# A graph kernel's first spreading: slot numbers of the even ranges as 8-bit bands

## The chip, the cores and the metric

The kernel runs on one NeuronCore of one Trainium2 chip. Its time is the device time of one execution in microseconds; of several executions the median is given. Changes of this kernel's time under about 0.2% are treated as no change.

## The reference, cut to what matters

Two layers of a graph network over N = 32768 nodes with D = 128 features and E = 524288 edges. The first layer sums the features of each edge's source at its destination; this sum is what the change touches:

```python
src, dst = (edge_index[0], edge_index[1])
agg = jax.ops.segment_sum(x[src], dst, num_segments=N)
h = (1.0 + eps) * x + agg
h = jax.nn.relu(h @ W_loc1 + b_loc1) @ W_loc2 + b_loc2
h_local = _bn(x + h, g1, beta1)
# beside it: attention of 8 heads over 64 blocks of 512 nodes, then a feed-forward part
```

The second layer does three steps of a retrieval (softmax over 512 keys) with a normalised sum over the same edges. Each layer ends in a layer norm.

## The kernel before, in words

**Ranges and slots.** The nodes are cut into NW = 256 ranges of 128. For each source range w and each of the 256 destination ranges there are KS = 6 slots, so a source range has SL = 2·6·128 = 1536 slots: 12 blocks of 128, six for each half of the destination ranges. A slot holds one edge, by the number (1 to 128) of the source node inside its range, or 0 for none. Edges that find no slot go through lists and are gathered elsewhere.

**Where the slot numbers are made.** `Grid.build` sorts the edges beside the first attention blocks and writes tables to memory: among them `row` of the key `dst`, 1536 slot numbers for each range, in bf16 (L816). For the other key, `src`, the same kind of table is written in 8 bits (`row2`, L824 to L826), and a later stage reads it.

**The stage of the change, `spread_x`.** It runs after the first 52 attention blocks and before a branch, from about 2375 us to 3625 us of the profiled span. The ranges are taken in order. For range w:

- Its one-hot `pick` is a 128 x 1536 tile: row p has a one where the slot number is p + 1. For an odd w the row of slot numbers is read from memory 128 times over, into all partitions (`band`, 384 KB, L1838), and VectorE compares the bf16 tile at once (`pick_b`, L1844). For an even w the row lies in SBUF (`row`, loaded once, L1371); TensorE copies 512 of it at a time to all partitions by a matmul with a column of the identity (`row_p`, L1423), and VectorE compares each of the three pieces from PSUM (`pick`, L1848).
- `spread` multiplies each 128 x 128 block of the one-hot with the 128 x 384 rows of the range (`rows`: x in three bf16 parts). For m = 0 to 5 two matmuls (L1448) fill a PSUM tile `exp` (three of these), and ScalarE or VectorE copies it to the SBUF tile `y_o` (L1453). VectorE has m = 2 of every range and m = 5 of the odd ones; ScalarE has the rest. There are two tiles `y_o`.
- After m = 2 and after m = 5 SyncE's queue issues a store of half the tile to `slots` (L1456, 576 KB each).

Every four ranges the next block of x is loaded (`xe`, L1826, 256 KB) and split in four small steps (L1395 to L1399), the last of which stores `rows`. Between the m of all ranges a share of a second sort is issued (`build_more`, `sort_on`): compares on VectorE, transposes on TensorE, copies on ScalarE. It has a quota in estimated time; its long compares end before 3300 us, and shorter steps follow until the end of the stage.

**Order.** The stage is under a manual schedule: each engine takes its instructions as the Python loop issues them, and waits only where a tile is not ready or not free. All loads and stores of the stage are on SyncE's queue, in issue order. Before the change the order in iteration w is: for odd w the load of the band of w + 2; every fourth w the load of x; and then for each m the two matmuls, the copy, a store after m = 2 and 5, and after m = 1, 3 and 5 one piece of the next range's `pick` (for an odd next range all of it after m = 1).

Of the kernel before, what the change touches and what calls it, by code (L numbers as in the profile page):

```python
# [9 lines left out]
F32 = mybir.dt.float32  # L10
I32 = mybir.dt.int32
BF16 = mybir.dt.bfloat16
FP8 = mybir.dt.float8e4
U8 = mybir.dt.uint8
AF = mybir.ActivationFunctionType
OP = mybir.AluOpType
# [4 lines left out]
P = 128  # L21
D = 128
BLK = 512
# [8 lines left out]
KS = 6  # L32
# [145 lines left out]
class Order:  # L178
# [10 lines left out]
    def __init__(self, tc, name, n, own, ident, iota, lane_f, dram, pool):  # L189
        nc = tc.nc  # L190
        self.tc, self.name, self.n = tc, name, n
        self.own, self.oth = (7, 0) if own == "src" else (0, 7)
        self.ident, self.iota, self.lane_f = ident, iota, lane_f
        self.NW = 2 * P
        self.F = n // P
        self.NS = self.F // self.SUB
        self.table = dram(f"sorted_{name}", (n + WL, 1), I32)
        self.pivots = dram(f"pivots_{name}", (P, self.NS), I32)
        self.begin = pool.tile([P, self.NW + 1], F32, name=f"begin_{name}")
        self.at = pool.tile([P, 2], I32, name=f"at_{name}")  # L200
# [233 lines left out]
class Grid:  # L434
# [18 lines left out]
    def __init__(self, tc, main, over, dram, pool):  # L453
        self.tc, self.main, self.over = tc, main, over
        NW = 2 * P
        self.out = {k: {"slot": dram(f"slot_{k}", (P, NW * self.NC2), BF16),
                        "other": dram(f"other_{k}", (P, NW * OW), I32),
                        "shared": dram(f"shared_{k}", (P, NW // GW * SH), I32),
                        "row": dram(f"row_{k}", (P, 2 * 2 * KS * P), U8 if k == "src" else BF16)}
                    for k in ("src", "dst")}  # L460
        self.more = dram("more", (P, 2, self.over.F // 2), I32)
        self.bad = pool.tile([P, self.NBAD], F32, name="bad")
        tc.nc.vector.memset(self.bad, 0.0)
        self.groups = pool.tile([P, P // GW], F32, name="groups")
        self.earlier = pool.tile([P, P], F32, name="earlier")
# [100 lines left out]
    def build(self, pp):  # L566

        tc, nc, PADL, NC2, Q, OL, LOW = self.tc, self.tc.nc, self.PADL, self.NC2, self.Q, self.OL, self.LOW
        main = self.main
        WS, OS = main.WSHIFT, main.OSHIFT  # L570
        mine, theirs = self.out["dst"], self.out["src"]
        NW = 2 * P
# [4 lines left out]
        with tc.tile_pool(name="gr", bufs=1) as sp:  # L577
# [16 lines left out]
            for h in range(2):  # L594
                with tc.tile_pool(name=f"gr_h{h}", bufs=1) as hp:
# [6 lines left out]
                    with tc.tile_pool(name=f"gr_a{h}", bufs=1) as ap:  # L602
# [13 lines left out]
                        w = ap.tile([P, 1], F32, name="w")  # L616
# [14 lines left out]
                                                op0=OP.is_gt)  # L631
# [50 lines left out]
                    with tc.tile_pool(name=f"gr_c{h}", bufs=1) as ap:  # L682
# [7 lines left out]
                        m = mask[:, :OL]  # L690
# [62 lines left out]
                        w = kept_w[:, :Q]  # L753
                        m = mask[:, :Q]
# [34 lines left out]
                        for b in range(10, -1, -1):  # L789
                            g = 1 << b  # L790
# [17 lines left out]
                        row = ap.tile([P, 2, KS, P], BF16, name="row")  # L808
                        for g in range(2):
# [6 lines left out]
                        nc.sync.dma_start(  # L816
                            mine["row"].rearrange("p (g h f) -> p g h f", g=2, h=2)[:, :, h, :],
                            row.rearrange("p g r w -> p g (r w)"))

                        half = ap.tile([P, KS, 2, P], BF16, name="half")  # L820
                        nc.scalar.copy(half.rearrange("p r g w -> p g r w"), vb)
# [88 lines left out]
def tile_gnn_resnorm(ctx: ExitStack, tc: tile.TileContext, a: dict, out: bass.AP):  # L910
# [8 lines left out]
    nc = tc.nc  # L919
# [3 lines left out]
    NW = N // P  # L923
# [5 lines left out]
    def dram(name, shape, dt=F32):  # L929
        return nc.dram_tensor(name, shape, dt, kind="Internal").ap()  # L930
# [17 lines left out]
    ident = cp.tile([P, P], F32, name="ident")  # L948
# [30 lines left out]
    w = {}  # L979
# [342 lines left out]
    SL = 2 * KS * P  # L1322
# [3 lines left out]
    gc = {}  # L1326
# [11 lines left out]
    def rows_of(t, i):  # L1338

        return t.rearrange("(b c p) d -> b p c d", c=NCH, p=P)[i]  # L1340
# [14 lines left out]
    class Exchange:  # L1355
# [10 lines left out]
            self.width = table.shape[1]  # L1366
            self.bands = {}

        def load_rows(self, pool):
            self.row = pool.tile([P, 2, SL], BF16, name="row")  # L1370
            nc.sync.dma_start(self.row.rearrange("p h f -> p (h f)"), self.grid["row"])  # L1371

        def load_tables(self, pool):

            self.slot = pool.tile([P, NW, NC2, 2], BF16, name="slot")
# [31 lines left out]
        def known_pick(self, wp, w):  # L1407
            pick = wp.tile([P, SL], FP8, name="pick", bufs=3)
            nc.sync.dma_start(pick, pick_d[w])
            return pick  # L1410

        def pick(self, wp, pp, tag, w):

            pick = wp.tile([P, SL], FP8, name="pick", bufs=3)
            for j in range(SL // BLK):
                nc.vector.tensor_scalar(pick[:, j * BLK:(j + 1) * BLK], self.listed_row(pp, tag, w, j), gc["lane1"],
                                        None, op0=OP.is_equal, saturate=False)
            return pick

        def listed_row(self, pp, tag, w, j):  # L1420

            ps = pp.tile([P, BLK], F32, name="row_p", tag=tag)
            nc.tensor.matmul(ps, gc["ident"][:, w % P:w % P + 1].to_broadcast([P, P]),  # L1423
                             self.row[:, w // P, j * BLK:(j + 1) * BLK], start=True, stop=True)
            return ps

        def load_band(self, wp, w):
            if w < NW:
# [383 lines left out]
    def spread_x():  # L1812

        ex = Exchange("dst", slots_d[1], rows_d[T_STEPS])
        with tc.tile_pool(name="l0r", bufs=1) as gp, tc.tile_pool(name="l0e", bufs=2) as wp, \
                tc.tile_pool(name="l0e_p", bufs=2, space=PSUM) as p_k, \
                tc.tile_pool(name="l0e_e", bufs=3, space=PSUM) as p_e:
            grid_consts(gp)
            ex.load_rows(gp)
            xb, rows, ends, picks, bands, y = {}, {}, {}, {}, {}, {}  # L1820
            more = {"steps": grid.build_more(lane, Bank(p_k, "row_p")), "quota": 0.0}

            def load(b):
                if b < NB:
                    xb[b] = wp.tile([P, NCH, D], F32, name="xe", bufs=3)
                    nc.sync.dma_start(xb[b], rows_of(a["x"], b))  # L1826

            def split(b):
                if b < NB:
                    x = xb.pop(b)  # L1830
                    rows[b], ends[b] = ex.split_steps(wp, b, x, x)

            def row_of(w):

                if w < NW:
                    bands[w] = wp.tile([P, SL], BF16, name="band")
                    src = ex.grid["row"][w % P:w % P + 1, w // P * SL:(w // P + 1) * SL]
                    nc.sync.dma_start(bands[w], src.to_broadcast([P, SL]))  # L1838

            def pick(w, j):  # L1840
                if w < NW and w % 2:
                    if j == 0:
                        picks[w] = wp.tile([P, SL], BF16, name="pick_b")
                        nc.vector.tensor_scalar(picks[w], bands.pop(w), gc["lane1"], None, op0=OP.is_equal)  # L1844
                elif w < NW:
                    if j == 0:
                        picks[w] = wp.tile([P, SL], FP8, name="pick")
                    nc.vector.tensor_scalar(picks[w][:, j * BLK:(j + 1) * BLK], ex.listed_row(p_k, "row_p", w, j),  # L1848
                                            gc["lane1"], None, op0=OP.is_equal, saturate=False)

            def sort_on():

                more["quota"] += MORE
                while more["steps"] is not None and more["quota"] > 0:
                    us = next(more["steps"], None)
                    if us is None:
                        more["steps"] = None
                    elif us < 0:
                        more["quota"] = 9 * us * MORE
                    else:  # L1860
                        more["quota"] -= us

            with tc.manual_schedule():
                load(0)
                load(1)
                split(0)
                for f in ends.pop(0):
                    f()
                row_of(1)
                for j in range(SL // BLK):  # L1870
                    pick(0, j)
                for w in range(NW):
                    b, c = divmod(w, NCH)
                    if w % 2:
                        row_of(w + 2)
                    if c == 0:
                        load(b + 2)
                        split(b + 1)
                    for m in range(KS):
                        ex.spread(wp, p_e, "exp", w, picks[w], rows[b][:, c, :], m, y, m == 2 or (m == 5 and w % 2))  # L1880
                        if m % 2:
                            pick(w + 1, m // 2)
                        if m == 3 and b + 1 in ends:
                            ends[b + 1][c]()
                        sort_on()
                for _ in more["steps"] or ():
                    pass
# [403 lines left out]
    with tc.tile_pool(name="atg", bufs=1) as gp, tc.tile_pool(name="ata", bufs=2) as ap, \  # L2291
# [4 lines left out]
        with tc.manual_schedule():  # L2296
# [13 lines left out]
            for us in edges or ():  # L2310
                pass
    spread_x()
    grid.verdict(flag)

# [47 lines left out]
```

## Time and profile before

| What | Value |
|---|---|
| Median of 3 runs | 13194.35 us (13187.15 to 13196.0) |
| Profiled execution, its own time | 13193.95 us |
| Its span in the profile | 13192.2 us, 164703 instructions |
| The stage `spread_x` in it | about 2375 to 3625 us |
| Mean granted TensorE clock | 0.946 |

The profile shows one execution. A group's row has its line, engine and operation, the tiles written and read, shapes and count, then the busy time in us and the mean of one in ns, and after the second bar the idle time of the engine just before it, with what ended most of that idle time. `PE` is TensorE, `PEld` its weight loads, `DVE` VectorE, `ACT` ScalarE, `POOL` GpSimd, `SP` SyncE. A row of a window has the stretch, its length, the busy time and count of each engine in the order PE, PEld, DVE, ACT, POOL, then the granted TensorE clock, the mean busy share of the 16 DMA engines, and GB/s.

### The profile page before, as it was taken

To read this page: it belongs to the slowest core of one execution; us is meant where nothing else is said; L and a number is where in the kernel's file an instruction comes from. 1 tells how busy PE (TensorE), PEld (TensorE's weight loads), DVE (VectorE), ACT (ScalarE), POOL (GpSimd) and SP (SyncE) were. 2 spreads that over 40 slices of the span, in tenths; PEclk is the share of its full clock that TensorE was granted. 3 is DMA by queue.
4 is the path that set the end of the run, shared out by engine and by line. 5 is a ranking of instruction groups with operands and counts; after the bars stand their busy time and mean duration, and the time that the engine had idled before them with its cause. 6 is when DMAs were issued, how large, how long until landed. Compare 5 with 4: busy or idle time off the path is not lost. (4 is left out here: it accounts for less than half of the span.)

```text
span 13192.2 us, 164703 instructions
## 1 busy us (share of the span) xinstructions
PE 11231.3 (85%) x57831; PEld 5536.4 (42%) x57831; DVE 9517.9 (72%) x15195; ACT 6589.1 (50%) x10238; POOL 6302.2 (48%) x5525
## 2 busy tenths in 40 slices
PE   7798798666679988889997999999899999866666
PEld 2233233232334444344443555555455555433333
DVE  7977977899777777678886666666566666566666
ACT  4455455677712222368885666666566666500000
POOL 0084075000077777300001666666566666477777
PEclk9999899999889999999999999999999999988888
DMA  1000000688899999778887999999999999988887
GB/s 43 10 15 19 10 14 16 252 321 323 324 307 316 322 319 320 254 259 309 305 311 293 396 400 400 399 397 397 352 400 398 396 401 399 363 299 290 289 290 255
DMA packets 1410558, 3689.71 MB, mean 280 GB/s; under 512 B 219827, under 2 KB 634707, under 8 KB 1408563
## 3 DMA queue, kind: packets, MB, share of 16 engines
q1 hardware_dynamic: 969712, 2969.23, 59.8%
q0 software_dynamic: 252608, 520.41, 12.5%
q10 hardware_dynamic: 187394, 189.42, 4.4%
q8 instruction: 457, 7.49, 0.2%
q14 instruction: 387, 3.16, 0.1%
HBM read 2175.76 MB, written 1502.58 MB: 279 GB/s over the span
## 5 line engine op out<-in xcount | busy, mean ns | idle before, releaser
L1470 POOL DMA_INDIRECT listed<-rows,other x5120 | 5291.4, 1033 | 4127.8 <-issue 3138.3
L1453 ACT CAST y_o<-exp 128x768 bf16<-128x768 f32 x4224 | 3234.0, 805 | 1162.2 <-PE exp L1448 784.7
L1495 PEld LDWEIGHTS <-oh 128*128 128x128 bf16 x19456 | 1970.8, 102 | 2570.0 <-issue 1529.6
L1448 PE MATMUL exp<-rows,pick 128*128 128x384 bf16 x10752 | 2426.5, 328 | 380.3 <-ACT y_o L1453 223.2
L1495 PE MATMUL seg<-y_i,oh 128*128 128x384 bf16 x12288 | 2563.4, 345 | 20.4 <-DMA y_i<-slots 19.7
L1453 DVE CAST y_o<-exp 128x768 bf16<-128x768 f32 x1920 | 1831.8, 954 | 690.5 <-PE exp L1448 559.1
L1495 PE MATMUL seg<-listed,oh 128*128 128x384 bf16 (+1 forms) x5120 | 1313.3, 335 | 801.7 <-DMA listed<-rows,other 780.5
L1448 PEld LDWEIGHTS <-pick 128*128 128x128 fp8e4 x10752 | 1045.7, 98 | 1729.8 <-issue 1162.7
L1661 ACT ACTIVATE pT<-s 128x1024 f32<-128x1024 f32 x1024 | 1048.4, 1025 | 1378.5 <-PE s L1636 957.5
L1641 DVE TENSOR_REDUCE mx<-s 128x2 f32<-128x1024 f32 x1024 | 1246.3, 1221 | 358.4 <-PE s L1636 357.9
L2179 DVE SCALAR_TENSOR_TENSOR part_i<-seg,dinv,part_i 128x128 f32<-128x128 f32 x1536 | 532.4, 347 | 1337.9 <-PE seg L1495 1319.2
L1657 PE MATMUL s<-ql,k 32*128 32x512 f32 x4096 | 1217.9, 673 | 167.8 <-DVE mx L1641 154.6
L1636 PE MATMUL s<-k,q 32*128 32x512 f32 x4096 | 1222.5, 676 | 9.3 <-DVE mx L1641 4.9
L1481 DVE TENSOR_TENSOR oh<-iota,slot 128x2432 bf16<-128x2432 bf16 x768 | 1087.3, 1416 | 3.0 <-DMA slots<-y_o 3.0
L1084 ACT ACTIVATE ln_rs<-ln_mv,eps_c 128x4 f32<-128x4 f32 x128 | 38.0, 297 | 1637.7 <-DVE ln_mv L1082 1637.7
L2104 PE MATMUL s<-keysT,qT 128*128 128x512 f32 x1536 | 793.7, 598 | 2.0 <-ACT pr L1063 1.4
L2116 PE MATMUL s<-pt,values 128*128 128x512 f32 x1536 | 720.4, 594 | 2.1 <-ACT pt L2111 2.0
L1495 PE MATMUL seg<-common,oh 128*128 128x384 bf16 (+1 forms) x2048 | 607.9, 350 | 50.9 <-DMA common<-rows,shared 50.8
L1657 PEld LDWEIGHTS s<-ql,k 32*128 32x128 f32 x4096 | 320.7, 191 | 763.2 <-DVE mx L1641 314.5
L1392 POOL MEMSET rows<- 128x8 bf16 x64 | 6.7, 106 | 1260.4 <-PE exp L1448 749.7
L1061 DVE TENSOR_REDUCE nm<-s 128x1 f32<-128x512 f32 x768 | 523.6, 684 | 105.6 <-PE s L2104 103.7
L1063 ACT ACTIVATE pr<-s,nm 128x512 f32<-128x512 f32 x768 | 536.3, 698 | 114.9 <-DVE nm L1061 112.1
(410 smaller groups left out, 14178.5 us busy)
## 6 DMA issues: line engine op xcount, KB each, us to landing
slots<-y_o SPq DMA_DIRECT2D x2048, 576.0 KB
y_i<-slots SPq DMA_DIRECT2D x1024, 1152.0 KB
pick<-pick SPq DMA_DIRECT2D x1024, 192.0 KB
listed<-rows,other POOLq DMA_INDIRECT x5120
rows<-rows SPq DMA_DIRECT2D x192, 384.0 KB
band<-row_dst SPq DMA_DIRECT2D x128, 384.0 KB
band<-row_src ACTq DMA_DIRECT2D x256, 192.0 KB
part_d<-part_o SPq DMA_DIRECT2D x192, 256.0 KB
```

Source lines behind the costliest of these rows:

```text
L1063: nc.scalar.activation(pr, s, AF.Exp, bias=nm, accum_out=sums)
L1448: nc.tensor.matmul(ps[:, j, :ROW], pick[:, o:o + P], r, start=True, stop=True)
L1453: (nc.vector.tensor_copy if to_dve else nc.scalar.copy)(dst, ps[:, :, :ROW])
L1470: nc.gpsimd.indirect_dma_start(out=g[:, k, :], out_offset=None, in_=self.table, in_offset=bass.IndirectOffsetOnAxis(ap=index[:, k:k + 1], ...
L1481: nc.vector.tensor_tensor(oh.rearrange("p c (w z) -> p c w z", z=2), ramp.rearrange("p (w z) -> p w z", z=2)[:, None].to_broadcast([P, NC2 ...
L1495: nc.tensor.matmul(ps[:, :n], oh[:, j, :], src, start=(k == 0), stop=(k == NC2 - 1))
L1636: nc.tensor.matmul(ps[:, s % 2, :], t["q", o][32 * s:32 * s + 32, c * P:(c + 1) * P], t["k", o][32 * s:32 * s + 32, :], start=True, stop=True)
L1641: nc.vector.tensor_reduce(m[:, c, 2 * i:2 * i + 2, xr[o]], st[b].pop(("two", i)), AX.X, OP.max, negate=True)
L1657: nc.tensor.matmul(ps[:, s % 2, :], t["k", o][32 * s:32 * s + 32, c * P:(c + 1) * P], t["ql", o][32 * s:32 * s + 32, :], start=True, stop= ...
L1661: nc.scalar.activation(t["p", c][:, 2 * i:2 * i + 2, :], ps, AF.Exp)
L2104: nc.tensor.matmul(s, st["q"][:, c * P:(c + 1) * P], keysT, start=True, stop=True)
L2116: nc.tensor.matmul(ps, values[:, k, :], st["pt"][:, k, :], start=(k == 0), stop=(k == NCH - 1))
```

## The change

The slot numbers of the key `dst` are also written in 8 bits: after `row` is stored, ScalarE copies it to an 8-bit tile `row8`, and SyncE's queue stores that (twice, once for each half of the ranges). In `spread_x` the even ranges read an 8-bit band from `row8` (192 KB, 128 x 1536), and VectorE compares it in one instruction into the fp8 one-hot. TensorE's broadcast, its SBUF table `row` and the three comparisons are gone. The odd ranges keep their bf16 band. Band w + 3 is now issued at the start of every iteration w, instead of band w + 2 at the start of the odd ones; the next range's comparison stands after m = 1 for all ranges; three bands are issued before the loop. The functions `load_rows`, `pick` and `listed_row` of `Exchange` are taken out.

```diff
+                        "row8": dram(f"row8_{k}", (P, 2 * 2 * KS * P), U8)}
...
+                        row8 = ap.tile([P, 2, KS, P], U8, name="row8")
+                        nc.scalar.copy(row8, row)
+                        nc.sync.dma_start(
+                            mine["row8"].rearrange("p (g h f) -> p g h f", g=2, h=2)[:, :, h, :],
+                            row8.rearrange("p g r w -> p g (r w)"))
...
-            ex.load_rows(gp)
...
-                    bands[w] = wp.tile([P, SL], BF16, name="band")
-                    src = ex.grid["row"][w % P:w % P + 1, w // P * SL:(w // P + 1) * SL]
+                    name, dt = ("row", BF16) if w % 2 else ("row8", U8)
+                    bands[w] = wp.tile([P, SL], dt, name="band_" + name)
+                    src = ex.grid[name][w % P:w % P + 1, w // P * SL:(w // P + 1) * SL]
                     nc.sync.dma_start(bands[w], src.to_broadcast([P, SL]))
...
-            def pick(w, j):
-                if w < NW and w % 2:
-                    if j == 0:
-                        picks[w] = wp.tile([P, SL], BF16, name="pick_b")
-                        nc.vector.tensor_scalar(picks[w], bands.pop(w), gc["lane1"], None, op0=OP.is_equal)
-                elif w < NW:
-                    if j == 0:
-                        picks[w] = wp.tile([P, SL], FP8, name="pick")
-                    nc.vector.tensor_scalar(picks[w][:, j * BLK:(j + 1) * BLK], ex.listed_row(p_k, "row_p", w, j),
-                                            gc["lane1"], None, op0=OP.is_equal, saturate=False)
+            def pick(w):
+                if w < NW:
+                    dt = BF16 if w % 2 else FP8
+                    picks[w] = wp.tile([P, SL], dt, name=f"pick{w % 2}")
+                    nc.vector.tensor_scalar(picks[w], bands.pop(w), gc["lane1"], None, op0=OP.is_equal,
+                                            **({} if w % 2 else {"saturate": False}))
...
-                row_of(1)
-                for j in range(SL // BLK):
-                    pick(0, j)
+                for i in range(3):
+                    row_of(i)
+                pick(0)
                 for w in range(NW):
                     b, c = divmod(w, NCH)
-                    if w % 2:
-                        row_of(w + 2)
+                    row_of(w + 3)
...
-                        if m % 2:
-                            pick(w + 1, m // 2)
+                        if m == 1:
+                            pick(w + 1)
```

More of the change, by code (lines that the diff above doesn't have):

```diff
@@ L458, in __init__ @@
                         "shared": dram(f"shared_{k}", (P, NW // GW * SH), I32),
-                        "row": dram(f"row_{k}", (P, 2 * 2 * KS * P), U8 if k == "src" else BF16)}
+                        "row": dram(f"row_{k}", (P, 2 * 2 * KS * P), U8 if k == "src" else BF16),
+                        "row8": dram(f"row8_{k}", (P, 2 * 2 * KS * P), U8)}
                     for k in ("src", "dst")}
@@ L1367, in __init__ @@
             self.bands = {}
-        def load_rows(self, pool):
-            self.row = pool.tile([P, 2, SL], BF16, name="row")
-            nc.sync.dma_start(self.row.rearrange("p h f -> p (h f)"), self.grid["row"])
         def load_tables(self, pool):
@@ L1410, in known_pick @@
             return pick
-        def pick(self, wp, pp, tag, w):
-            pick = wp.tile([P, SL], FP8, name="pick", bufs=3)
-            for j in range(SL // BLK):
[L1416 to L1425, printed above, removed]
         def load_band(self, wp, w):
@@ L1868, in spread_x @@
                     f()
-                row_of(1)
-                for j in range(SL // BLK):
-                    pick(0, j)
+                for i in range(3):
+                    row_of(i)
+                pick(0)
                 for w in range(NW):
                     b, c = divmod(w, NCH)
-                    if w % 2:
-                        row_of(w + 2)
+                    row_of(w + 3)
                     if c == 0:
```

## The prediction

> **What bounds the stage now.** The page comes first: VectorE is busy 72% of the span, TensorE 85%, and no engine all the time, so the stage must be read by itself. I asked for the groups of 2375 to 3625 us, the stage (line, shapes, count, then busy us and mean ns, then idle us before it and what ended it):
>
> ```profile
> L1453 ACT CAST y_o<-exp 128x768 bf16<-128x768 f32 x1152 | 862.1, 811 | 306.9 <-PE exp L1448 158.5 <-DMA slots<-y_o 127.3 <-DVE begin_over L330 3.6
> L1453 DVE CAST y_o<-exp 128x768 bf16<-128x768 f32 x384 | 365.3, 951 | 18.1 <-DMA slots<-y_o 11.0 <-PE exp L1448 5.4 <-ACT y_o L1453 0.7
> L1848 DVE TENSOR_SCALAR pick<-row_p,lane 128x512 fp8e4<-128x512 f32 x384 | 286.3, 746 | 87.0 <-PE row_p L1423 86.2
> L1423 PE MATMUL row_p<-row,ident_b 128*128 128x512 bf16 x382 | 159.1, 416 | 9.7 <-DVE pick L1848 9.6
> L1844 DVE TENSOR_SCALAR pick_b<-band,lane 128x1536 bf16<-128x1536 bf16 x128 | 78.9, 616 | 41.5 <-DMA band<-row_dst 40.9
> ```
>
> The three comparisons of an even range take 3 x 0.746 = 2.24 us of VectorE, the single one of an odd range 0.62. ScalarE waits 127 us for stores that have not landed, since there are two tiles `y_o`. That is a first sign of the DMA.
>
> Then the stage by windows. The first stretch has the second sort's long compares on VectorE, the other two have no sort; each begins and ends at a `pick_b`, so they hold 76, 4 and 8 pairs of ranges:
>
> ```profile
> core 0: us, PE busy (x) PEld busy (x) DVE busy (x) ACT busy (x) POOL busy (x), PEclk, DMA share, GB/s
> 2470.87:3199.89 729.02, 488.87 (x2278) 225.16 (x2279) 682.50 (x833) 554.55 (x789) 4.01 (x38) 0.96 0.89 322
> 3319.45:3355.77 36.32, 25.34 (x112) 10.92 (x110) 24.00 (x33) 29.07 (x42) 0.21 (x2) 0.95 0.93 342
> 3534.24:3608.02 73.78, 52.28 (x223) 22.81 (x222) 48.09 (x65) 58.75 (x84) 0.32 (x3) 0.90 0.90 331
> ```
>
> This decides my reading. In the first stretch VectorE is 94% busy and looks like the bound. But a pair takes 729.02 / 76 = 9.59 us with 8.98 us of VectorE, and in the others (36.32 + 73.78) / 12 = 9.18 us with 6.01 us of it. Taking 2.97 us from VectorE gave 0.42 us: 0.14 for each. The DMA's share stays near 0.9. So the pair is set by a loop: two tiles `y_o`, each filled by copies and emptied by stores that queue on 16 DMA engines already nine tenths busy.
>
> **Cost on the DMA.** The change adds 128 bands of 128 packets of 1536 bytes, 16384 packets, 25.2 MB (it drops one load of 0.8 MB). The page's queues give the price of a packet:
>
> ```profile
> q1 hardware_dynamic: 969712, 2969.23, 59.8%
> q10 hardware_dynamic: 187394, 189.42, 4.4%
> ```
>
> q1: 0.598 x 16 x 13192 us / 969712 = 130 ns at a mean of 3062 bytes. q10: 0.044 x 16 x 13192 / 187394 = 50 ns at 1011 bytes. The line through both gives 70 ns at 1536 bytes: 16384 x 70 / 16 engines = 72 us. By bytes at the stage's 320 GB/s it is 79 us. The far end is q1's whole 130 ns, 133 us, since all partitions read the same row of memory. I take 75 us, next to the two near ones. The stage's DMA work is now 0.88 x 1250 = 1100 us; it becomes 1175.
>
> **Cost and gain on VectorE.** No row of this trace has an 8-bit comparison without an accumulator. The nearest two:
>
> ```profile
> L1438 DVE TENSOR_SCALAR_CACHE_REDUCE pick<-band,lane 128x1536 fp8e4<-128x1536 uint8 x256 | 459.9, 1796 | 20.3 <-DMA band<-row_src 20.2
> L428 DVE TENSOR_SCALAR val<-m 128x896 int32<-128x896 int32 x2 | 1.2, 624 | 0.0
> ```
>
> The first has the same operands and writes a sum too: 1.80 us, one element a cycle. The second is without a sum, from SBUF to SBUF in types that are not two bytes wide: 896 in 624 ns, 0.70 ns each, or 1.07 us for 1536. I take 1.07 us, as this comparison has no sum, with 1.80 as the other end. The gain is 2.24 - 1.07 = 1.17 us a pair, 150 us over 128 pairs (0.44 us and 56 us at the other end). At 0.14 for each us it is worth 21 us of time.
>
> The Trainium skill, in "VectorE: DVE Perf Modes", section on the perf-mode tier table, has `tensor_scalar` at two elements a cycle where source and destination lie in SBUF and are not all 16 bits wide, and less from PSUM. By that rule the comparison takes about the 1.07 us of the second row; the first row alone would have said 1.80.
>
> **Waits taken and added.** The 86.2 us that VectorE waits for `row_p` go; at the same 0.14 they give 12 us. The 40.9 us for the bf16 bands should go too: band w + 3 is issued two ranges before its comparison where it was one, about 9.6 us against 4.8, and the longest wait is 3.8 us; 6 us at 0.14. The comparison of an even range now waits for a band; behind it on VectorE stand the copy of m = 2 and the sort, and behind that copy SyncE's store. With the lead of two ranges it waits for nothing; without it, up to 3.8 us each time. On SyncE's queue each pair has one more issue, 0.4 to 0.9 us in front of a store; SyncE waits 695 us in the stage for VectorE's copies, which hides it, and uncovered it would be 64 us at 0.5 us each. All gains sum to about 39 us, if DMA work were free; it isn't, since 75 us go into the resource that sets the loop.
>
> **TensorE** loses 384 matmuls (159 us), off the chain where its clock is full. But its clock falls when it has little to do:
>
> ```profile
> 3433.00:3434.00 1.00, 0.00 (x0) 0.00 (x0) 1.00 (x2) 1.00 (x3) 0.00 (x0) 1.00 1.03 416
> 3434.00:3435.00 1.00, 0.00 (x0) 0.00 (x0) 0.93 (x4) 0.23 (x1) 0.00 (x0) 1.00 1.01 408
> 3436.00:3437.00 1.00, 1.00 (x5) 0.60 (x5) 0.00 (x0) 0.37 (x1) 0.00 (x0) 0.50 1.08 413
> ```
>
> These are single microseconds: two with no matmul and the DMA full, then half the clock. The two stretches without sort had clocks of 0.95 and 0.90 and 9.08 and 9.22 us a pair, 0.14 us for 0.05. If the stage's 0.93 falls to 0.90, that is 0.08 us a pair, 11 us. I leave it inside the range.
>
> The skill's "TensorE: Matmul & The Clock Gate", Part 1, says that the clock is halved after an idle window of about 3.4 us. It speaks against taking work from TensorE; here gaps of some 2.5 us were enough, and by the trace's price it is the same 11 us.
>
> **Elsewhere.** Two ScalarE copies of 1536 into 8 bits in the attention stage. The nearest row, L825 (1536 from f32 to 8 bits), takes 2953 ns; three of L1399's 512 (629 ns) are 1.9 us. TensorE waited for ScalarE behind L825, so between 0 and 6 us; I take 4. Their two stores lie beside attention. At the start the first comparison now waits for a band issued at 2383 us where it began at 2382.4; but range 1 waited for its band until 2388.4 anyway, so 0 to 4 us, and I take 2.
>
> **The sum.** The stage's time is DMA work over the share it reaches. Now: 1100 / 0.88 = 1250. After, VectorE is relieved about halfway to the stretches without sort, whose shares are 0.93 and 0.90. I take 0.915: 1175 / 0.915 = 1284, 34 us more, in which the 39 us of relief are contained (without any it would be 1175 / 0.88 = 1335, 85 more). With 4 and 2 it is +40 us. Against the profiled execution's 13193.95 us (span 13192.2 and 1.75 around it, 0.4 under the median) that gives 13234 us. The stage breaks even, with the 6 us, at a share of 1175 / 1244 = 0.945.
>
> **Rivals.** About 0.2%, 26 us, is what a measurement of this kernel can tell from no change.
>
> *VectorE was the bound (faster).* For it: 94% busy in 800 us, and picks and waits of 150 + 86 + 41 us go. Against it: the 0.14. The time then falls until the DMA stops it. At a share of 0.97, near the 1.0 of single microseconds, the stage takes 1211 us: with 6 us, 13161. It decides from a share of 0.945 on.
>
> *The gaps swallow the bands (no change).* The DMA idles 12% of the stage, 150 us, and half of that would do. For it: an 8-bit band is issued at the start of the odd ranges, between two stores. Share 0.94, stage 1250: 13200.
>
> *The 8-bit comparison runs at one element a cycle, or the packets cost 130 ns (clearly slower).* So the change doesn't give VectorE what it says: 0.44 us a pair at L1438's price. Share 0.90 with 1175 gives 1306, +62: 13256. With dear packets 1233 / 0.90 = 1370, +126: 13320.
>
> **How the numbers follow.** The forecast, slower by 26 us to about 60, has 0.47; the clearly slower one 0.15; together slower 0.62. No change has 0.22, faster 0.16. The slopes come from two short stretches and may miss by half, hence the chances on the other side. The range leaves out a tenth on each side: from 13155, six below the faster rival's time, to 13305, between the two prices of the last rival.
>
> **What would show it.** Right: the stage some 30 us longer; a DMA share of 0.91 to 0.92 in it; VectorE's busy time about 150 us less and more of its idle time ended by stores or by `exp`; more of ScalarE's wait ended by `slots`; 8-bit bands at 65 to 85 us of the engines. Wrong: a comparison near 1.8 us; bands that VectorE waits for; the attention stage or a later one changed by over 10 us. If the stage gets shorter with the DMA at 0.95 or more, my step from 0.14 to "DMA-bound" failed.

## The result and the profile after

The changed kernel takes 13219.81 us (median of 17 runs, 13200.98 to 13239.21), the kernel before 13193.44 us in the 17 runs beside it: a ratio of 1.0019, 95% interval 1.0012 to 1.0027, so slower by 16 to 36 us. The forecast was 13234 us. Both kernels were profiled twice, the second time in experiments 11 and 12.

| | before | before, second profile | after | after, second profile |
|---|---|---|---|---|
| First load of x for the stage (attention's work is issued) | 2376.3 | 2375.8 | 2382.5 | 2380.2 |
| First spreading matmul | 2383.6 | 2383.2 | 2395.8 | 2393.4 |
| Stage, first to last spreading matmul | 1238.6 | 1234.0 | 1255.7 | 1258.7 |
| DMA work in it (sum of the packets' times / 16), us | 1093.9 | 1091.6 | 1158.3 | 1167.7 |
| DMA share | 0.883 | 0.885 | 0.922 | 0.928 |

The span grew by 20.5 us (13192.2 to 13212.7). By the first pair of profiles that is +6.2 us before the stage, +6.1 between the first load and the first matmul, +17.1 in the stage, and 9 us that came back later. The span of one kernel differs between executions by as much (14 us between before's two profiles, 18 between after's), so the 9 us are given no cause. The stage repeats within 5 us in both pairs.

The groups of the stage after the change (2375 to 3655 us; line, engine, tiles, shapes, count, then busy us and mean ns, then idle us before them and what ended it):

```profile
L1440 ACT CAST y_o<-exp 128x768 bf16<-128x768 f32 x1152 | 861.2, 814 | 334.7 <-DMA slots<-y_o 237.3 <-PE exp L1435 82.7 <-DVE more_a L96 3.6
L1435 PE MATMUL exp<-rows,pick 128*128 128x384 bf16 x3072 | 772.3, 377 | 465.1 <-ACT y_o L1440 330.0 <-DVE y_o L1440 100.1 <-DVE pick L1831 21.4
...
L1440 DVE CAST y_o<-exp 128x768 bf16<-128x768 f32 x384 | 366.5, 954 | 280.2 <-PE exp L1435 141.5 <-DMA slots<-y_o 113.0 <-ACT y_o L1440 21.1
...
L1831 DVE TENSOR_SCALAR pick<-band_row,lane 128x1536 fp8e4<-128x1536 uint8 x128 | 129.5, 1012 | 6.5 <-DMA band_row<-row_dst 6.5
L1831 DVE TENSOR_SCALAR pick<-band_row,lane 128x1536 bf16<-128x1536 bf16 x128 | 78.3, 612 | 0.3 <-DMA band_row<-row_dst 0.3
```

VectorE no longer waits for its inputs: the 86 us for `row_p` and the 41 us for bands are gone but for one wait of 6.35 us at the start. But it waits 113 us for stores, where it was 11, and 141 us for `exp`, where it was 5; ScalarE's wait for stores went from 127 to 237 us. And TensorE waits for copies of `y_o`, 330 us for ScalarE's and 100 for VectorE's. Before the change these were 226 and 98 us (both kinds of one-hot together):

```profile
L1448 PE MATMUL exp<-rows,pick_b 128*128 128x384 bf16 x1536 | 382.0, 350 | 204.3 <-ACT y_o L1453 144.0 <-DVE y_o L1453 57.5 <-DVE w L861 0.2
L1448 PE MATMUL exp<-rows,pick 128*128 128x384 bf16 x1536 | 366.1, 345 | 179.0 <-ACT y_o L1453 82.0 <-DVE y_o L1453 40.3 <-DVE rows L1395 39.1
```

So VectorE's longer wait for `exp` looks like the same wait handed on: its freed time has become waiting in the loop of `y_o`.

The whole stage by a window, before and after (length, then busy time and count of PE, PEld, DVE, ACT and POOL, then granted clock, DMA share, GB/s):

```profile
2383.60:3622.20 1238.60, 830.69 (x3722) 375.42 (x3721) 1081.70 (x1477) 928.36 (x1317) 12.27 (x68) 0.93 0.88 321
```

```profile
2395.80:3651.50 1255.70, 798.25 (x3339) 364.85 (x3340) 952.07 (x1221) 926.78 (x1317) 13.60 (x68) 0.86 0.92 336
```

VectorE's busy time fell by 129.6 us, and the stage is 17.1 us longer. In the 76 pairs with the second sort's compares a pair went from 9.59 to 740.73 / 76 = 9.75 us, with VectorE at 606.32 us, 82% where it was 94%:

```profile
2482.71:3223.44 740.73, 473.74 (x2042) 221.97 (x2043) 606.32 (x682) 551.88 (x785) 4.01 (x38) 0.87 0.93 336
```

The queue that carries all the stage's loads and stores has 18832 more packets in the whole program, 16384 of them the new bands (packets, MB, share of 16 engines):

```profile
q1 hardware_dynamic: 988544, 2994.01, 60.1%
```

### The profile page after: what moved, and what is told of

It is laid out like the page before. It is cut to its first block, busy times and chain, and to the rows that moved or that the text cites. A ratio compares the mean times of both kernels' runs of the same rounds, so it can differ in the third digit from the quotient of the medians.

```text
span 13212.7 us, 163752 instructions
## 1 busy us (share of the span) xinstructions
PE 11211.1 (85%) x57447; PEld 5537.9 (42%) x57447; DVE 9384.4 (71%) x14939; ACT 6585.7 (50%) x10240; POOL 6306.1 (48%) x5525
## 5 line engine op out<-in xcount | busy, mean ns | idle before, releaser
L1435 PE MATMUL exp<-rows,pick 128*128 128x384 bf16 x12288 | 2832.7, 338 | 663.9 <-ACT y_o L1440 469.3
L1435 PEld LDWEIGHTS <-pick 128*128 128x128 fp8e4 (+1 forms) x12288 | 1226.4, 100 | 2220.7 <-issue 1651.8
```

Of the source, the lines that this page charges most:

```text
L1435: nc.tensor.matmul(ps[:, j, :ROW], pick[:, o:o + P], r, start=True, stop=True)
```

## The experiments

The theory of the prediction was that the loop of two tiles `y_o` through the DMA queues sets the pace, and VectorE's time hardly matters. The main rival was that VectorE was the bound. Experiments 1 to 4 ran together on a chip where the whole program takes some 8% longer, nearly all of it in later stages, so their totals are given as ratios to the kernel before on that same chip. The kernel before was not profiled there, so their stages are compared with its profiles from elsewhere. By the ratios the totals differ from it by about 53, -27, 43 and 131 us, and by the profiles the stages by 34, -32, 37 and 122 us. All stage lengths go from the first to the last spreading matmul of one profile.

**1. Even ranges from a bf16 band.** The 8-bit table is still written and not read.

```diff
-name, dt = ("row", BF16) if w % 2 else ("row8", U8)
+name, dt = "row", BF16
```

> The changed kernel, with the even ranges' bands read in bf16 (384 KB) in place of 8 bits (192 KB), still compared in one instruction; the 8-bit table is still written. DMA work +83 us (16384 packets, 88 to 169 ns in the changed kernel's trace), VectorE -52 us (128 x 0.40 us). Theory (the DMA sets the stage, a us of VectorE is worth 0.14): 83 / 0.92 = +90 - 7, so about 83 us over the changed kernel, 13303 us. Rival (VectorE sets it): 52 us under the changed kernel, 13168 us. Rival (the loss comes from the order of issue and from the start, not from bytes): as the changed kernel, 13220 us.

Measured: ratio 1.0037 (1.0021 to 1.0052). Its stage:

```profile
2399.10:3671.70 1272.60, 825.93 (x3340) 374.55 (x3340) 954.25 (x1221) 927.42 (x1317) 13.67 (x68) 0.82 0.96 351
```

It took 1272.6 us, 17 more than after (14 more than its second profile), for 1216.0 us of DMA work, 58 more; the share rose to 0.956. The forecast of 83 us was far too high: most of the added work went into gaps. VectorE's work did not fall as expected (954.3 us against 952.1): into the fp8 one-hot the comparison takes 1.014 us from a bf16 band too, not 0.61. So the run adds DMA work alone and does not test the rival with VectorE. The idea of a share that VectorE's relief sets does not hold.

**2. The relief without the bands.** All even ranges compare one band that is loaded once, so 127 loads are left out.

```diff
+held = gp.tile([P, SL], U8, name="held")   # loaded once, from row8
-nc.vector.tensor_scalar(picks[w], bands.pop(w), ...)
+nc.vector.tensor_scalar(picks[w], bands.pop(w) if w % 2 else held, ...)
```

> The changed kernel, with one 8-bit band loaded once and compared for every even range: the loads of the other 127 8-bit bands are left out, so the even ranges' slot numbers are not those of the reference. VectorE's work is unchanged, DMA work -90 us. Theory (DMA): stage of (1157 - 90) / 0.92 = 1160 us, 95 under the changed kernel, 13125 us; by the prediction's slope of 0.14 the relief alone would be worth 39 us and the time 13167 us. Rival (the bands lie in gaps of the DMA, the loss is order and start): 13220 us.

Measured: ratio 0.9981 (0.9966 to 0.9996). Its stage:

```profile
2397.50:3604.00 1206.50, 793.10 (x3339) 355.93 (x3340) 949.19 (x1221) 919.50 (x1317) 14.00 (x68) 0.87 0.90 329
```

132.5 us less of VectorE than before, and no broadcast by TensorE, bought 32.1 us: 0.24 for each. VectorE was not a bound whose relief would pay in full. And the bands in the changed kernel cost 1255.7 - 1206.5 = 49 us, half of the theory's 95 and not the rival's nothing.

**3. The bands without the relief.** The kernel before, which also loads the 8-bit bands and never reads them.

```diff
 if w % 2:
     row_of(w + 2)
+elif w + 2 < NW:
+    band8 = wp.tile([P, SL], U8, name="band8")
+    nc.sync.dma_start(band8, ex.grid["row8"][...].to_broadcast([P, SL]))
```

> The kernel before, with the 8-bit table written and an 8-bit band loaded for every even range that nobody reads: the change's DMA work (90 us) without its relief of VectorE and TensorE. Theory (DMA, share stays at 0.88 to 0.92): +60 to +102 us in the stage and 4 before it, 13260 to 13300 us. Rival (the gaps swallow the bands): 13198 us.

Measured: ratio 1.0030 (1.0018 to 1.0042). Its stage:

```profile
2395.30:3671.00 1275.70, 848.30 (x3658) 384.30 (x3721) 1083.94 (x1477) 924.47 (x1317) 12.27 (x68) 0.91 0.93 331
```

It took 1275.7 us, 37 us more than before, for 90 us more of DMA work (1184.1), at a share of 0.928. The prediction had 85 us for this case. So the share goes from 0.88 to 0.93 by the transfers alone, with VectorE as busy as ever: over half of the work fits where the DMA idled.

**4. More work for VectorE.** The kernel before, with the comparison of each odd range issued three times.

```diff
+nc.vector.tensor_scalar(picks[w], bands[w], gc["lane1"], None, op0=OP.is_equal)
+nc.vector.tensor_scalar(picks[w], bands[w], gc["lane1"], None, op0=OP.is_equal)
 nc.vector.tensor_scalar(picks[w], bands.pop(w), gc["lane1"], None, op0=OP.is_equal)
```

> The kernel before, with the comparison of every odd range done three times: +158 us of VectorE's work (256 x 0.617), as much as the change takes from it; nothing else moves. Theory (a us of VectorE is worth 0.14): +22 us, 13216 us. Rival (VectorE, 94% busy, is the bound while the sort lasts): +100 us or more, 13294 us and over.

Measured: ratio 1.0092 (1.0072 to 1.0112). Its stage:

```profile
2386.70:3746.90 1360.20, 898.11 (x3659) 388.21 (x3721) 1234.17 (x1733) 936.30 (x1317) 12.40 (x68) 0.86 0.81 292
2483.13:3287.14 804.01, 532.24 (x2243) 234.97 (x2279) 772.42 (x986) 560.37 (x789) 4.01 (x38) 0.88 0.81 292
```

152.5 us more of VectorE cost 121.6 us, 0.80 for each, and the DMA's share fell to 0.81. The rival's number was right and the slope of 0.14 wrong. With experiment 2 this is the main finding: around the kernel before, a microsecond of VectorE costs 0.80 when it is added and gives 0.24 when it is taken away (there together with TensorE's broadcast).

It is not only that VectorE was full. In the 76 pairs with the sort (second row) 89.9 us more of VectorE cost 75.0 us, 0.83 for each. In the rest of the stage, where the kernel before has VectorE busy 399.2 of 509.6 us, 78%, 62.6 us cost 46.6, still 0.75. The added comparisons stand in front of the next one-hot, and TensorE waits for it:

```profile
L1448 PE MATMUL exp<-rows,pick_b 128*128 128x384 bf16 x1535 | 427.3, 386 | 206.2 <-DVE pick_b L1846 91.3 <-ACT y_o L1453 78.8 <-DVE y_o L1453 23.8
```

In the kernel before the waits for `pick_b` in this row were at most 0.2 us. So VectorE's work lay on the path that sets the pace, and the next bound lay right under it. What that is, the third tile tells.

**5. All bands in 8 bits.** The table of `dst` is written in 8 bits at once; there is no bf16 table and no second copy, and odd ranges too are compared in 8 bits.

```diff
-row = ap.tile([P, 2, KS, P], BF16, name="row")
+row = ap.tile([P, 2, KS, P], U8, name="row")
-name, dt = ("row", BF16) if w % 2 else ("row8", U8)
+name, dt = "row", U8
```

> All bands in 8 bits, and the table written in 8 bits at once, so without the extra ScalarE copies: DMA work -83 us against the changed kernel, VectorE +52 us (128 x 0.40 us). The stage is counted from the first to the last matmul of the spreading; it was 1238.6 us before and 1255.7 us after. Theory (VectorE and the DMA are both near the bound; by the first four runs a us of DMA work is worth 0.3 to 0.5, one of VectorE 0.2 to 0.77): -25 to -42 and +10 to +40, stage 1224 to 1270 us. Rival (DMA alone): 1075 / 0.922 = 1166 us. Rival (VectorE alone): 1295 us.

Measured: 13176.62 us, ratio 0.9982 (0.9972 to 0.9991). Its stage:

```profile
2404.00:3600.60 1196.60, 786.79 (x3340) 358.29 (x3340) 997.08 (x1221) 925.04 (x1317) 13.57 (x68) 0.88 0.92 331
```

It took 1196.6 us, 59 less than after and shorter than the forecast's whole range, though longer than the 1166 of the rival with the DMA alone. VectorE has 45 us more than after (997.1), which costs nothing visible, and the DMA 63 us less. It is 10 us shorter than experiment 2 at nearly the same DMA work (1095.0 and 1087.5). Its bands are 192 KB every range where that one has 384 KB every second; that the smaller transfers hold up the stores less is only argued.

**6. The same with another start.** The first three bands are issued before the second load of x, and the first comparison before the end of the split.

```diff
 load(0)
+for i in range(3):
+    row_of(i)
 load(1)
 split(0)
-for f in ends.pop(0):
-    f()
-for i in range(3):
-    row_of(i)
 pick(0)
+for f in ends.pop(0):
+    f()
```

> As the run with all bands in 8 bits, and the first three bands issued before the second load of x, and the first comparison before the split of the second block. The first comparison waited 6.4 us for its band in the changed kernel's trace: the first spreading matmul comes about 6 us earlier after the last attention block, the stage itself as in the run without this.

Measured: 13162.23 us, ratio 0.9974 (0.9965 to 0.9984). From the first load of x to the first matmul it takes 7.3 us, where experiment 5 had 12.0 and the kernel before 7.3. The stage is the same, 1200.3 us. The matmul began 20 us earlier than in experiment 5, but 15 of these lie before the first load, in code that the two share.

**7 and 8. A third tile `y_o`**, in the changed kernel and in the kernel before.

```diff
-st["y"] = wp.tile([P, 2, KS, ROW], BF16, name="y_o")
+st["y"] = wp.tile([P, 2, KS, ROW], BF16, name="y_o", bufs=3)   # in spread_x
```

> The changed kernel with three tiles y_o in the first spreading in place of two. Theory (a loop of two tiles holds the stage; ScalarE and VectorE wait 237 and 113 us for stores in the changed kernel): those waits shrink to under 100 us and the DMA share rises to 0.96 or more, stage 1206 us or less, 50 us faster. Rival (the engines' own work sets it): within 10 us of 1255.7.

> The kernel before with three tiles y_o in the first spreading. Theory (VectorE is the nearer bound there, busy 1178 of 1238.6 us, and the loop of two tiles costs the rest): 10 to 30 us faster, stage 1210 to 1229 us, so the third tile brings less here than in the changed kernel. Rival (the loop alone holds both kernels): as much as there, 50 us.

Measured: the changed kernel with three tiles 13075.54 us, ratio 0.9906 (0.9890 to 0.9923); the kernel before with three 13185.73, ratio 0.9987 (0.9977 to 0.9996). First the changed kernel's stage and its groups:

```profile
2407.60:3503.10 1095.50, 740.27 (x3339) 340.39 (x3340) 943.93 (x1221) 916.48 (x1317) 13.72 (x68) 0.94 1.01 385
```

```profile
L1440 ACT CAST y_o<-exp 128x768 bf16<-128x768 f32 x1152 | 852.4, 817 | 183.8 <-PE exp L1435 121.9 <-DMA slots<-y_o 46.6 <-DVE y_o L1440 10.2
...
L1440 DVE CAST y_o<-exp 128x768 bf16<-128x768 f32 x384 | 365.2, 951 | 34.8 <-PE exp L1435 25.1 <-ACT y_o L1440 4.5 <-ACT shared L532 2.6
...
L1831 DVE TENSOR_SCALAR pick<-band_row,lane 128x1536 fp8e4<-128x1536 uint8 x128 | 130.0, 1016 | 79.1 <-DMA band_row<-row_dst 78.7
```

The same work in 160 us less: ScalarE's wait for stores falls from 237 to 47 us, VectorE's from 113 to almost nothing, and by its packets' times the DMA is full (share 1.01); now the 8-bit bands are late. Then the kernel before with three tiles:

```profile
2399.70:3617.30 1217.60, 834.88 (x3660) 372.43 (x3720) 1076.29 (x1477) 930.17 (x1318) 12.49 (x68) 0.93 0.90 326
2487.97:3205.04 717.07, 499.82 (x2239) 225.92 (x2276) 680.04 (x833) 555.02 (x788) 4.05 (x38) 0.94 0.90 327
```

```profile
L1453 ACT CAST y_o<-exp 128x768 bf16<-128x768 f32 x1152 | 860.6, 808 | 278.7 <-PE exp L1448 194.9 <-issue 65.4 <-ACT y_o L1453 13.8
...
L1844 DVE TENSOR_SCALAR pick_b<-band,lane 128x1536 bf16<-128x1536 bf16 x128 | 79.2, 619 | 75.2 <-DMA band<-row_dst 75.0
```

ScalarE's large waits are none of them for stores now, yet the stage is only 21 us shorter (16 by the second profile of the kernel before). The 65 us that the row puts down to `issue` are 33 waits, nearly all of which end about 0.6 us after a late spreading matmul began; in 24 of them that matmul had waited for `rows`, the split of x, whose last step is VectorE's. In the 76 pairs with the sort (second row) VectorE is busy 680 of 717 us, 95%: there it is the bound, as experiment 4 said. So the same edit gives 160 us after the change and 21 before it. The changed kernel is held by two tiles; with three, the change itself is worth 1217.6 - 1095.5 = 122 us of the stage, nearly all of the 132 us that VectorE gave up. Of this 78 us lie in the 76 pairs with the sort (717.1 us, and 639.6 with the change) and 45 in the rest, where VectorE was busy only 79% of the time. The change also takes TensorE's 384 broadcast matmuls and VectorE's wait for them away. No run takes these away alone, so what share of the 122 us is theirs stays open.

**9 and 10. The variants together:** experiment 6 with three tiles, and the changed kernel with three tiles and the new start.

> All bands in 8 bits, the first three bands issued before the second load of x, and three tiles y_o. With three tiles the changed kernel's DMA engines were full (1108.8 us of work in a stage of 1095.5); all bands in 8 bits take 50 to 65 us of it. Theory (with three tiles the DMA is the bound): stage 1040 to 1050 us. Rival (VectorE, 1073 us of work, is the next bound): stage 1085 to 1105, no gain over the changed kernel with three tiles but the 12 us of the start. In both cases faster than the kernel before, 13040 to 13075 us.

> The changed kernel with three tiles and the first three bands issued before the second load of x; the odd ranges' bands stay in bf16. Against the run with all bands in 8 bits beside it, it shows what the bf16 bands cost once the DMA is full: 50 us if the DMA is the bound, nothing if VectorE is. About 12 us less than the three tiles alone, 13064 us.

Measured: all in 8 bits 13064.40 us, ratio 0.9901 (0.9884 to 0.9917); with the bf16 bands 13069.70, ratio 0.9904 (0.9887 to 0.9920). The stages are 1092.0 and 1102.2 us. The theory's 1040 to 1050 us did not come; the rival, VectorE as the next bound, had 1085 to 1105. With three tiles the 8-bit bands bring only 10 us, not the 59 that they brought with two, nor the 50 of a full DMA. The 76 pairs with the sort, of the kernel that is all in 8 bits:

```profile
2464.41:3107.98 643.57, 431.25 (x2044) 205.47 (x2043) 626.44 (x681) 545.09 (x786) 4.05 (x38) 0.96 0.99 364
```

VectorE is at 97% and the DMA at 0.99 at once, so moving work from one to the other should win little more; no run tries it. This kernel is about 131 us faster than the kernel before, and 155 faster than the changed one by their medians on different chips.

**11 and 12. Both kernels once more**, for the spread of the stage.

> The kernel before once more, for how far the length of the stage varies between profiled executions: 1238.6 us in the first; if it lies within 6 us, the differences of 17 us and more that were read from single profiles stand.

> The changed kernel once more, for the same: 1255.7 us in the first profile.

Measured: 13180.04 and 13232.79 us, one run each; their stages stand in the first table. The difference of the stage is 24.7 us in this pair, 17.1 in the first, so 17 to 25 us is what the stage cost.

## Why the prediction was right, and where it was wrong

**The sum.** Forecast +40 us: 34 in the stage, 4 for the copies, 2 for the start. Measured +26 by the medians; in the two pairs of profiles +17 to +25, +4 to +6 and +6. The sign and the place were right, and the stage's term came out at half to three quarters of its size. Its two parts were further off. The prediction charges 85 us for the bands without relief and takes off 51 by the share of 0.915 (its own list of gains has 39, and the two are not reconciled). Measured were 49 and 32 us by experiment 2, or 37 and 20 by experiment 3. Both parts were too large and the errors cancelled in part, and the measured 26 us lie at the lower edge of the forecast's 26 to 60. So the near agreement was in part luck.

**DMA work.** 75 us forecast; 64 us in one pair of profiles and 76 in the other. The 8-bit packets took 88 ns, not 70, or 90 us of the engines, a little above the 65 to 85 that I had named; in the first pair the others became cheaper beside them (3072 bytes from 175 to 169 ns, the stores' 4608 from 190 to 186).

**The comparison.** 1.07 us forecast, 1.012 measured. The row without a sum was the right neighbour and the 1.80 us of the row with one was not. The Trainium skill's "VectorE: DVE Perf Modes", perf-mode tier table, gives `tensor_scalar` on fp32 in SBUF twice the rate of 1×. The trace agrees as far as it goes: 0.66 ns for each 8-bit element and 0.70 in int32, against 1.17 where a sum is written too. The gain was 129.6 us and not 150. By means and counts the comparisons of the even ranges fell by 286.3 - 129.5 = 157 us. But records that follow each other on VectorE overlap by about 0.08 us, 97 us in the stage before and 69 us after, where there are 256 fewer. A mean duration times a count overstated the engine's time, and the windows, which merge overlaps, did not.

**The slope of 0.14.** As the price of relief it was near: 39 us forecast for what experiment 2 measured as 32. As a reading of what bounds the kernel it was half of the truth. It compares a stretch where VectorE was nearly full with stretches where it had a third of its time free, so it shows what lies below the bound. For added work the slope is 0.80 (experiment 4). The stretch with the sort, at 94%, was bound by VectorE, and "looks like the bound" was dismissed too fast. Nor did the two short stretches stand for the stage: the 40 pairs that lie in none of the three took 399.5 / 40 = 9.99 us with 327.1 / 40 = 8.18 us of VectorE, longer than the pairs with the sort and with less of VectorE.

**Stage = DMA work over a share.** This is the step that failed. It made the share depend on VectorE's relief and priced the bands without relief at 85 us; experiment 3 measured 37, with the share at 0.928 and no relief. The price of DMA work was also no constant: 0.41 for each us in experiment 3 (37 of 90), 0.69 between experiment 2 and the changed kernel (49 of 71), 0.29 from there to experiment 1 (17 of 58). That 0.915 was nearly the measured 0.922 and 0.928 was partly chance. What sets the pace of the changed kernel, as the third tile shows, is the round trip of a `y_o` tile: filled by six copies, then stored behind whatever is in the queues. That more DMA work lengthens the store's part of it, and a freer VectorE hardly shortens the copies' part, is how I read it and not shown by itself. Why the price differs as it does stays open.

**Waits.** All as forecast: `row_p` 86 us to none, bf16 bands 41 to 0.3, 8-bit bands none after the first, ScalarE's idle time ended by `slots` up by 110 us, VectorE's ended by stores or `exp` up by 238.

**TensorE's clock.** 0.90 was allowed for; 0.86 and 0.83 came. With the same matmuls the kernel with three tiles has 0.94, so it is not the loss of 384 matmuls alone. TensorE's waiting for `y_o` (430 us after the change, 324 before) does not explain it alone either: experiment 4 has 0.86 with 240 us of it. By the prediction's price of 11 us for 0.03, a fall of 0.07 would be 26 us, more than the stage lost. But experiments 2 and 5 had 0.87 and 0.88 in stages 32 and 42 us shorter than before, so a low clock does not by itself make the stage long. No run separates it from the waiting, and it stays open. The gaps of 2.5 us that the prediction names are a round figure: the one in its lines lasted 3.0 us, and one from 3409.6 to 3411.4 us, 1.8 us long, was followed by half the clock as well.

**The start.** 2 us forecast, 6 measured at the first matmul. From the timeline of the kernel before, SyncE's queue (`SPq`) and VectorE (start, length, what; idle time before it in brackets):

```profile
2382.43 2.17 DVE L1848 TENSOR_SCALAR pick<-row_p,lane 128x512 fp8e4<-128x512 f32 x3
2382.58 0.34 SPq L1396 DMA_DIRECT2D rows<-rows  x1
2382.97 0.42 SPq L1838 DMA_DIRECT2D band<-row_dst  x1
```

And from that of the changed one:

```profile
2388.44 0.34 SPq L1398 DMA_DIRECT2D rows<-rows  x1
...
2388.83 1.92 SPq L1825 DMA_DIRECT2D band_row<-row_dst  x4
...
2394.72 1.02 DVE L1831 TENSOR_SCALAR pick<-band_row,lane 128x1536 fp8e4<-128x1536 uint8 x1 [6.35 <-DMA band_row<-row_dst]
```

The bands stand behind the store of `rows`, which waits for the split of x. Before the change that cost little, since the first comparison took its row from SBUF. In fourteen profiles the first load of x came 7.1 to 7.9 us ahead of the first matmul where the kernel had the old order or experiment 6's, and 12.0 to 13.4 us where it had the changed kernel's. The first band is issued as long after the first load of x as before (6.4 and 6.7 us). The prediction had this wait, and set against it that range 1 waited for its band anyway. That held: the first matmul of range 1 came 13.6 us after the first load in both profiles before, and 17.2 and 17.0 after, so by then only 3.5 of the 6 us were left. The stage, counted from the first matmul, holds the other 2.5 us as a gain, and the forecast of 0 to 4 us was fair.

**The copies.** They take 1.47 us each, not 1.9. The attention stage ended 4 to 6 us later, as forecast, but the moment of the first load lies anywhere from 2376 to 2395 us in the fourteen profiles: 2392 in experiment 5 and 2377 in 6, whose attention code is one and the same. So the 4 us are neither shown nor refuted.

**The rivals.** The gaps that swallow the bands were closer than I gave them: over half of the bands' work went into gaps in experiment 3 and a third in the changed kernel, and 1250 us was forecast for the 1256 to 1259 measured. The interval of the ratio, 1.0012 to 1.0027, takes in that bound of 0.2%. VectorE as the bound was true for the kernel before in the pairs with the sort, and yet its relief did not pay, because the loop of two tiles took over after 32 us (experiment 2). The dear comparison did not come.

## What to carry to other kernels

When two bounds lie close together, the slope for added work and the slope for removed work differ (here 0.80 and 0.24), and a slope read between two stretches of one trace tells only one of them: add to the suspected engine's work and also take it away. When an engine is relieved and its idle time is then ended by the stores of its own output tiles, give that loop another tile before judging the change (here +17 us of the stage became -122 us). A moved load starts where its queue lets it, so read what is issued ahead of it in the new order, and count to the first step that had to wait in both orders (here 6 us at the first matmul were 3.5 at range 1).

## What the runs showed of the hardware that I had not expected

The time of a packet is not set by its size: the 8-bit bands' packets of 1536 bytes took 88 ns in the changed kernel, 114 beside an unrelieved VectorE (experiment 3), and 70 with three tiles, where the DMA was fullest. Those are means; the median was 65 ns in all three. A mean share of 1.01 of the DMA engines was held over the whole stage with three tiles, at 385 GB/s against 321 before, and 1.02 over its 76 pairs with the sort, at 390. The granted TensorE clock fell from 0.93 to 0.86 when TensorE lost 384 matmuls and waited more, and came to 0.94 with the same matmuls and a third tile.
